# Two half quotients of a dynamic-convolution softmax, issued two places later in a hand-written schedule

## The chip, the cores and the metric

The kernel runs on one core of one Trainium2 chip. The metric is device time in microseconds (us) for one execution; lower is better. The core's engines are PE (TensorE, matmuls), DVE (VectorE), ACT (ScalarE), POOL (GpSimd) and SP (SyncE, which issues the DMAs here). Each engine works through its own list of instructions in order and waits on semaphores for the others.

## The reference

The input is x, 8 images of 256 channels by 64 x 64 pixels, fp32. Two layers follow each other, each x = x + conv(groupnorm(x)). Layer 0 is an involution: per pixel, a small network makes 9 weights for each group of 8 channels, and they weigh the pixel's 3 x 3 neighbourhood. Layer 1 adds two parts. One is attention of every pixel over its 7 x 7 neighbourhood, 4 heads, with a softmax over the 49 keys. The other is a dynamic convolution:

```python
wts = jnp.einsum('oc,bchw->bohw', Wfc, x).reshape(b, C, kc2, h, w)
wts = jax.nn.softmax(wts, axis=2)
...
out_conv = jnp.sum(oc * wts.transpose(0, 2, 1, 3, 4), axis=1)
return rate1 * out_att + rate2 * out_conv
```

All 9 branches of `oc` hold the same values, since x is broadcast over them. The weighted sum is therefore `oc` times the sum of the softmax over its 9 branches; the kernel computes that as a quotient, (the sum of 8 exponentials of differences, plus 1) times the reciprocal of the same sum.

## The kernel before, in words

**Tiling.** An image is cut into 8 bands (g counts them through all images: image b = g // 8, band i = g % 8) of 8 rows, 512 pixels. Channels lie on partitions, in two tiles of 128 (ct = 0, 1). Layer 1's work on a band is cut into 8 steps: step s has ct = s // 4 and m = s % 4. In each step the kernel

- computes attention scores of two 8 x 8 tiles of queries on PE (`scores`, L703), takes them out of PSUM with mask and maxima on DVE (L712), makes exponentials with their sums on ACT (`exponentials`, L720), inverts the sums on DVE (`probabilities`, the *small reciprocal*, L727, 128 x 2 elements) and scales the probabilities on ACT (L729);
- transposes the probabilities of the step before on PE (`transposed`, L735), copies them on ACT (L737), and multiplies those of two steps before with the values (L747); DVE adds the result to the residual (L757);
- computes two of the eight 1 x 1 convolutions for the dynamic weights on PE (`branch_weights`, L825) and their exponentials on ACT (L830); POOL sums them up (L1023);
- runs four taps of two depthwise convolutions on DVE (L782 of the first, L808 of the second; ACT starts and ends them, L773, L788, L802, L818).

Beside these, spread over the steps: the queries, keys and values of coming bands (`queries` L637, `keys` L658 with sums on DVE at L666 and L673 and a copy of old rows on POOL at L633, `values` L563, `value_tile` L607 and L609), and layer 0 some 12 bands ahead (`small_maps` L328, `value_maps` L369, `hidden_maps`, `tap_weights` with one product on DVE, L460, and one sum on POOL, L468, for each of the 9 taps).

**Order.** The order on every engine is written by hand: nothing reorders it. The main loop passes six *places* a step. `advance()` moves to the next place and runs what was put there with `after(n, f)`, n places on. In a step, the first place comes after the scores and exponentials are issued, the second after the first branch convolution and two taps, the third after the small reciprocal and the scaling, the fourth after two more taps, the fifth after the second branch convolution, the sixth after the work that is kept for the end of a step (layer 0's products are put there relative to it).

**The quotients.** When the four steps of one ct are done (at m = 3), `dynamic_sum` is put four places on, which is the second place of the next step. It adds the two halves of the exponentials' sum (L838) and 1 to it (L841) on POOL, into the tile `tot`. The quotient is made in two halves of 256 elements: DVE takes the reciprocal (`quotient`, L846) into `rec`, and one place later POOL multiplies (L847). `rec` is one buffer, which both halves use. Then `weigh` multiplies with the depthwise result and adds to the residual on POOL (L851, L852), and six places after the second ct the band is stored. For the last band's ct = 1 all of this is on DVE.

Counted in places from `dynamic_sum`, at the second place of a step with m = 0, the first half stands 7 on: the third place of the step with m = 1, just behind the small reciprocal. The second half stands 11 on: the first place of the step with m = 2. For ct = 0 these are steps 5 and 6 of the same band, for ct = 1 steps 1 and 2 of the next.

Of the kernel before, what the change touches and what calls it, by code (L numbers as in the profile page):

```python
# [86 lines left out]
def conv_layers_kernel(ctx: ExitStack, tc: tile.TileContext, ins: dict, out: bass.AP):  # L87
# [127 lines left out]
    def after(n, f):  # L215
        later.append((place[0] + n, f))
# [615 lines left out]
    def dynamic_sum(b, i, ct, ex, oc):  # L832

        tot = w1.tile([P, BAND], F32, tag="tots", name=f"tot_{b}_{i}_{ct}", bufs=1)
        xr = images[b].xr[i]

        engine = nc.vector if (b, i, ct) == (B - 1, NB - 1, NCT - 1) else nc.gpsimd
        engine.tensor_add(tot, ex[:, 1], ex[:, 0])  # L838


        engine.tensor_scalar(tot, tot, 1.0, 1.0e37, ALU.add, ALU.min)  # L841
        rec = w1.tile([P, BAND // 2], F32, tag="rec", name=f"rec_{b}_{i}_{ct}", bufs=1)

        def quotient(u):
            v = tot[:, u * BAND // 2 : (u + 1) * BAND // 2]
            nc.vector.reciprocal(rec, v)  # L846
            after(1, lambda: engine.tensor_mul(v, v, rec))  # L847

        def weigh():

            engine.tensor_mul(oc, oc, tot)  # L851
            engine.tensor_add(xr[:, ct], xr[:, ct], oc)  # L852
            if ct == NCT - 1:
                after(6, store)

        def store():
            nc.sync.dma_start(
                out=out[b].rearrange("(t p) n -> p t n", p=P)[:, :, i * BAND : (i + 1) * BAND], in_=xr
            )

        after(7, lambda: quotient(0))
        after(11, lambda: quotient(1))
        after(13, weigh)


    def beside(g, s):
# [93 lines left out]
    with tc.manual_schedule():  # L960
# [21 lines left out]
        for g in range(-AHEAD, B * NB):  # L982
            b, i = divmod(g, NB)
            for s in range(STEPS):
# [35 lines left out]
                if g >= 0:  # L1020
                    branch_weights(b, i, ct, m, 1, ex)
                    if exb is not None:
                        after(4, lambda ex=ex, exb=exb: nc.gpsimd.tensor_add(ex, ex, exb))  # L1023
                    if m == 1:
                        conv[1]()
                        conv = depthwise_middle(b, i, ct)
                    if m == NT // 2 - 1:
                        oc = depthwise_end(b, i, ct, conv[1])
                        after(4, lambda a=(b, i, ct, ex, oc): dynamic_sum(*a))
# [97 lines left out]
```

## Time and profile before

| what | value |
|---|---|
| runs shown | 4149.93 us median of 3, 4146.99 to 11589.33 |
| the profiled execution | 4146.57 us, of which the span of its instructions 4144.8 us |
| busy share of PE, DVE, ACT, POOL | 97%, 82%, 75%, 76% |
| the half quotients L846 | 256 of 1742 ns, DVE idle 123.7 us ahead of them |
| the small reciprocals L727 | 512, median 159 ns |
| POOL's multiplies L847 | 254 of 730 ns, POOL idle 326.6 us ahead of them |
| granted clock of PE, mean | 0.990 |

A group's row of the page reads: line, engine, operation, what it writes and reads, how many | busy us, mean ns of one | idle time of its engine just before, and what ended most of it. A row of the waits reads: who waited, for whom, total us, times, longest us. A row of the order of time reads: start in us from the span's start, duration, engine, line, and in brackets the engine's idle time before it. A row of the windows reads: stretch, its length, then busy us and instructions of PE, PE's weight loads, DVE, ACT and POOL, then PE's granted clock, the DMAs' share and GB/s. PE's starts are measured and its ends are modelled, so its gaps are best read from start to start.

### The profile page before, as it was taken

Reading aid. Unit: us, or ns where it says so; the run is one execution under the profiler, and the core shown is the slowest. Engines: PE = TensorE matmul, PEld = TensorE weight load, DVE = VectorE, ACT = ScalarE, POOL = GpSimd, SP = SyncE. Lnnn points to the kernel's source line nnn. Section 1 sums busy time; section 2 is a strip of 40 time slices with the busy share of each in tenths; the row PEclk is TensorE's granted clock in tenths of the full one; section 3 lists DMA queues with packets and bytes.
Section 4 is the critical chain, followed back from the end, with each engine's and each line's share of the span. In section 5 each row is a group of like instructions: output and inputs, shape, how many; then the busy total and the mean of one; then the engine's idle time right before and its main releaser. Section 6 shows DMA issues by size and latency. Waiting matters only on the chain.

```text
span 4144.8 us, 72568 instructions
## 1 busy us (share of the span) xinstructions
PE 4025.7 (97%) x25292; PEld 2134.1 (51%) x25292; DVE 3414.6 (82%) x7090; ACT 3092.9 (75%) x7758; POOL 3170.8 (76%) x2156
## 2 busy tenths in 40 slices
PE   6889999999999999999999999999999999999998
PEld 2345555555555555555555555555555555555554
DVE  5778888788888888888888888888888788877777
ACT  3467778778777777877778777777778777687776
POOL 4768888788887888878887878878888788855555
PEclk9999999999999999999999999999999999999999
DMA  8853333333343433433433433342433332111100
GB/s 225 193 138 89 95 91 96 83 97 88 84 100 81 103 94 78 100 96 82 98 85 83 105 97 81 89 103 77 99 84 81 79 90 73 41 46 39 39 28 21
DMA packets 381262, 367.87 MB, mean 89 GB/s; under 512 B 55648, under 2 KB 282720, under 8 KB 380640
## 3 DMA queue, kind: packets, MB, share of 16 engines
q1 hardware_dynamic: 377568, 358.68, 34.6%
q8 instruction: 200, 3.28, 0.3%
q10 hardware_dynamic: 3328, 4.55, 0.3%
q14 instruction: 166, 1.36, 0.1%
HBM read 261.42 MB, written 101.71 MB: 88 GB/s over the span
## 4 chain that ended last, share of the span: by engine, by line
PE 44%; POOL 21%; DVE 19%; ACT 7%; issue 5%; DMA 2%; SPq 2%; POOLq 0%; DVEq 0%; ACTq 0%
PE pf L825 20%; POOL xg L468 9%; DVE rec L846 6%; POOL ex L1023 5%; DVE prod L460 5%; PE sco L747 3%; PE pk L658 3%; PE ptp L735 3%; PE sco L703 3%; PE p L369 2%; PE pq L637 2%; DVE acc L782 2%; DVE acc L808 2%; POOL tot L841 2%; PE pvt L607 2%
## 5 line engine op out<-in xcount | busy, mean ns | idle before, releaser
L825 PE MATMUL pf<-yp,c_wfc 128*128 128x512 f32 x4096 | 1935.2, 596 | 11.0 <-ACT vc L581 5.3
L468 POOL TENSOR_TENSOR xg<-xg,prod 128x1024 f32<-128x1024 f32 x549 | 1200.8, 2187 | 377.6 <-DVE prod L460 357.6
L825 PEld LDWEIGHTS pf<-yp,c_wfc 128*128 128x128 f32 x4096 | 733.2, 191 | 693.4 <-issue 596.8
L1023 POOL TENSOR_TENSOR ex<-ex,ex 128x1024 f32<-128x1024 f32 x384 | 908.0, 2365 | 110.0 <-ACT ex L830 105.8
L782 DVE SCALAR_TENSOR_TENSOR acc<-yp,c_chan,acc 128x504 f32<-128x504 f32 (+3 forms) x1104 | 765.2, 693 | 48.7 <-ACT acc L773 28.2
L460 DVE SCALAR_TENSOR_TENSOR prod<-pw,c_par,x3q 128x1040 f32<-128x1040 f32 x576 | 733.0, 1279 | 69.4 <-PE pw L447 24.6
L808 DVE SCALAR_TENSOR_TENSOR acc<-hid,c_chan,acc 128x504 f32<-128x504 f32 (+3 forms) x1024 | 756.7, 739 | 18.1
L830 ACT ACTIVATE ex<-pf 128x512 f32<-128x512 f32 x1024 | 604.1, 590 | 207.3 <-PE pf L825 192.4
L729 ACT ACTIVATE prob<-prob,tot 128x196 f32<-128x196 f32 x1024 | 411.9, 452 | 356.1 <-DVE tot L727 356.0
L712 DVE CUSTOM_DVE_ANT_0 prob<-sco,c_mask 128x196 f32<-128x196 f32 x1024 | 326.3, 356 | 272.4 <-PE sco L703 271.4
L846 DVE RECIPROCAL rec<-tot 128x256 f32<-128x256 f32 x256 | 446.1, 1742 | 123.7 <-POOL tot L841 123.7
L720 ACT ACTIVATE prob<-prob,nmax 128x196 f32<-128x196 f32 x1024 | 461.1, 454 | 16.4 <-DVE nmax L712 14.9
L847 POOL TENSOR_TENSOR tot<-tot,rec 128x256 f32<-128x256 f32 x254 | 185.5, 730 | 326.6 <-DVE rec L846 326.6
L747 PEld LDWEIGHTS sco<-pt,vt 112*64 112x64 f32 x8160 | 283.9, 137 | 182.1 <-issue 62.8
L737 ACT COPY pt<-ptp 112x512 f32<-112x512 f32 x511 | 296.2, 580 | 105.3 <-PE ptp L735 102.1
L747 PE MATMUL sco<-pt,vt 112*64 112x64 f32 x8160 | 347.4, 227 | 0.0
L735 PE MATMUL ptp<-ident,prob 128*112 128x128 f32 x2044 | 339.8, 288 | 6.7 <-ACT prob L729 5.8
L703 PE MATMUL sco<-kb,qb 64*64 64x196 f32 x4096 | 296.7, 359 | 0.0
L735 PEld LDWEIGHTS ptp<-ident,prob 128*112 128x112 f32 x2044 | 206.6, 134 | 169.4 <-issue 94.9
L841 POOL TENSOR_SCALAR tot<-tot 128x512 f32<-128x512 f32 x127 | 243.6, 1918 | 11.1
L563 PE MATMUL pv<-yp,c_wv 128*128 128x512 f32 (+2 forms) x576 | 246.8, 553 | 0.0
L369 PE MATMUL p<-xc,w3s 128*128 128x512 f32 x512 | 244.8, 602 | 0.0
(140 smaller groups left out, 5165.1 us busy)
## 6 DMA issues: line engine op xcount, KB each, us to landing
x<-x3n SPq DMA_DIRECT2D x128, 264.0 KB, 2.1
x3q<-x SPq DMA_DIRECT2D x128, 264.0 KB, 7.4
xc<-in_x SPq DMA_DIRECT2D x64, 512.0 KB, 5.2
xg<-in_x SPq DMA_DIRECT2D x256, 128.0 KB, 5.1
x<-xg SPq DMA_DIRECT2D x256, 128.0 KB, 2.4
yp<-x SPq DMA_DIRECT2D x128, 256.0 KB, 3.3
xr<-x SPq DMA_DIRECT2D x64, 512.0 KB, 6.1
out_x<-xr SPq DMA_DIRECT2D x64, 512.0 KB, 3.1
```

Of the source, the lines that this page charges most:

```text
L460: nc.vector.scalar_tensor_tensor(prod[:, :, :RUN], pw[:, j, :RUN].unsqueeze(1).to_broadcast([P, SHARE, RUN]), par[:, PCB2 + k : PCB2 + k + 1],
L468: nc.gpsimd.tensor_add(im.xg[i], im.xg[i], rows(prod))
L703: nc.tensor.matmul(sco[half[t], h, :NKEY], qb[half[h], 2 * m + t].rearrange("p r c -> p (r c)"), kb[half[h], :, c0 : c0 + KW], start=True, ...
L720: nc.scalar.activation(prob[:, h, :NKEY], prob[:, h, :NKEY], AF.Exp, bias=nmax[:, h : h + 1], scale=-1.0, accum_out=tot[:, h : h + 1],)
L735: nc.tensor.transpose(ptp[:, h, ch], prob[:, h, ch * CHUNK : (ch + 1) * CHUNK], ident)
L747: nc.tensor.matmul(po[half[h], :, t * TQ : (t + 1) * TQ], im.vt[i + ch, m][:n, t, (2 * ct + h) * HD : (2 * ct + h + 1) * HD], pt[:n, h, ch ...
L782: nc.vector.scalar_tensor_tensor(o, yp[:, ct, ra + dr : rb + dr, ca + dc : cb + dc], chan[:, ct, CW1 + k : CW1 + k + 1], o, ALU.mult, ALU.add,
L808: nc.vector.scalar_tensor_tensor(o, hid[:, ra + dr : rb + dr, ca + dc : cb + dc], chan[:, ct, CW2 + k : CW2 + k + 1], o, ALU.mult, ALU.add,)
L825: nc.tensor.matmul(pf, wfc[:, kt, 2 * m + j, ct * P : (ct + 1) * P], images[b].yp[i][:, kt, PAD : PAD + R], start=(kt == 0), stop=(kt == N ...
L830: nc.scalar.activation(ex[:, j].rearrange("p (r c) -> p r c", r=R), pf, AF.Exp)
L846: nc.vector.reciprocal(rec, v)
L1023: after(4, lambda ex=ex, exb=exb: nc.gpsimd.tensor_add(ex, ex, exb))
```

## The change

The first half goes from 7 to 9 places, the second from 11 to 13, and `weigh` from 13 to 15. The first half is then issued after the last two taps of the step with m = 1, the second after the small reciprocal of the step with m = 2.

```diff
-        after(7, lambda: quotient(0))
-        after(11, lambda: quotient(1))
-        after(13, weigh)
+        after(9, lambda: quotient(0))
+        after(13, lambda: quotient(1))
+        after(15, weigh)
```

On DVE, in a step with m = 1 and the one with m = 2 behind it:

```
before                                    after
L727 small reciprocal (m = 1)             L727 small reciprocal (m = 1)
L846 half quotient 0                      L782 taps, 2
L782 taps, 2                              L846 half quotient 0
L460 product (where one stands)           L460 product (where one stands)
L712 mask and maxima, L757 (m = 2)        L712 mask and maxima, L757 (m = 2)
L846 half quotient 1                      L460 product (where one stands)
L460 product (where one stands)           L808 taps, 2
L808 taps, 2                              L727 small reciprocal (m = 2)
L727 small reciprocal (m = 2)             L846 half quotient 1
L808 taps, 2                              L808 taps, 2
```

## The prediction

> **What bounds the kernel now.** I read the page first (busy shares, costliest groups), then who waited for whom, then PE's order of time in single steps, last DVE's and ACT's order of time ahead of PE's gaps. In the names below image b and band i count from 0, and a band has steps 0 to 7 (step s is ct = s // 4, m = s % 4).
>
> ```profile
> PE 4025.7 (97%) x25292; PEld 2134.1 (51%) x25292; DVE 3414.6 (82%) x7090; ACT 3092.9 (75%) x7758; POOL 3170.8 (76%) x2156
> L846 DVE RECIPROCAL rec<-tot 128x256 f32<-128x256 f32 x256 | 446.1, 1742 | 123.7 <-POOL tot L841 123.7
> ACT prob L729 <- DVE tot L727: 356.0, 267, 3.2
> PE pvt L607 <- ACT ex L830: 14.6, 6, 2.4
> ```
>
> PE is the bound: 97% busy, and DVE, ACT and POOL have 18 to 25% to spare. So an edit on DVE is worth only what it takes out of PE's few gaps. The second line says that DVE stood still 123.7 us ahead of the half quotients, waiting for POOL's sum; the third that ACT's scaling of the probabilities waited 356 us for the small reciprocal (L727); the fourth that PE waited six times, 2.4 us each, for an exponential of ACT.
>
> The same step (step 7, one of band 4, one of band 3 of image 3) with and without a gap, PE's order of time, start and duration:
>
> ```profile
> 2051.07 0.58 PE L703 MATMUL sco<-kb,qb 64*64 64x196 f32 x8
> 2051.78 0.78 PE L735 MATMUL ptp<-ident,prob 128*112 128x128 f32 x4
> 2052.70 1.98 PE L825 MATMUL pf<-yp,c_wfc 128*128 128x512 f32 x4
> 2054.52 1.88 PE L658 MATMUL pk<-yp,c_wk 128*128 128x512 f32 x4
> 2059.97 0.57 PE L703 MATMUL sco<-kb,qb 64*64 64x196 f32 x8
> ...
> 1990.68 0.58 PE L703 MATMUL sco<-kb,qb 64*64 64x196 f32 x8
> 1991.18 0.65 PE L735 MATMUL ptp<-ident,prob 128*112 128x128 f32 x4
> 1991.67 1.88 PE L825 MATMUL pf<-yp,c_wfc 128*128 128x512 f32 x4
> 1998.83 0.57 PE L703 MATMUL sco<-kb,qb 64*64 64x196 f32 x8
> ```
>
> From score to score the first takes 8.90 us, the second 8.15 us, with the same instructions. The 0.75 us lie around the transposes L735, which need the probabilities of step 6: 0.21 us ahead of them, 0.43 us between their halves, 0.10 us after. What DVE and ACT did just before the slow one:
>
> ```profile
> 2039.16 0.16 DVE L727 RECIPROCAL tot<-tot 128x2 f32<-128x2 f32 x1
> 2041.79 1.75 DVE L846 RECIPROCAL rec<-tot 128x256 f32<-128x256 f32 x1 [2.48 <-POOL tot L841]
> 2043.46 1.46 DVE L782 SCALAR_TENSOR_TENSOR acc<-yp,c_chan,acc 128x512 f32<-128x512 f32 x2
> 2044.83 1.29 DVE L460 SCALAR_TENSOR_TENSOR prod<-pw,c_par,x3q 128x1040 f32<-128x1040 f32 x1
> 2046.86 1.74 DVE L846 RECIPROCAL rec<-tot 128x256 f32<-128x256 f32 x1
> 2048.52 1.20 DVE L460 SCALAR_TENSOR_TENSOR prod<-pw,c_par,x3q 128x1040 f32<-128x1040 f32 x1
> 2051.08 0.16 DVE L727 RECIPROCAL tot<-tot 128x2 f32<-128x2 f32 x1
> ...
> 2051.27 0.81 ACT L729 ACTIVATE prob<-prob,tot 128x196 f32<-128x196 f32 x2 [3.12 <-DVE tot L727]
> ```
>
> The first half quotient holds DVE for 2.48 us with two ready taps behind it; the second stands ahead of the small reciprocal; ACT waits 3.12 us for that one, and PE's transposes wait for ACT. The chain that ended last has these same pieces (rec L846 is 6% of it).
>
> [...] the taps at 2043.46 needed nothing and stood behind the waiting reciprocal. [...]
>
> ```profile
> 2235.26 0.65 PE L607 MATMUL pvt<-ident,vc 128*112 128x128 f32 x4 [2.42 <-ACT ex L830]
> 2230.50:2235.20 4.70, 2.34 (x10) 1.08 (x8) 4.66 (x10) 1.53 (x5) 3.28 (x3) 1.00 0.00 0
> 2237.20:2241.20 4.00, 4.00 (x13) 2.15 (x10) 3.96 (x10) 1.63 (x6) 3.84 (x4) 0.66 0.00 0
> ```
>
> The column after the five engines is the granted clock: 0.66 just after the gap. [...] The moved reciprocal reads one, and POOL's L468 takes 2.17 to 2.19 us beside it and away from it; I cost contention at nothing.
>
> **The change part by part.** The built order shows that PE, ACT and SP keep their instructions in the same order (so every DMA issue too). On DVE only the 256 half quotients move; on POOL the second multiply (L847) goes behind the copy of keys L633 where one stands there. Nothing is added or removed.
>
> *First half.* It goes from ahead of two taps to behind them, still ahead of the product L460. In steps 5 the taps (1.46 us) run in what was a wait: 2.48 - 1.46 leaves a wait of 1.0 us, and everything behind (product, mask, scores' maxima of step 6) comes up to 1.46 us earlier. In steps 1 DVE did not wait for POOL, the sum is the same, and nothing behind moves. POOL's first multiply then ends later by 1.46 us in steps 1, but the next thing in POOL's queue, the sum L468, waits for the product, which takes 1.29 us against the multiply's 0.73: nothing.
>
> *Second half.* It goes behind the product, two taps and the small reciprocal: 1.74 us less ahead of L727. L727 cannot run before ACT's exponentials end. They ended 3.5 us before it in steps 6, 1.8 us in steps 2 (from the order of time), so the whole 1.74 us comes in steps 6, about 1.65 in steps 2. Together L727 of step 6 comes about 3.2 us earlier, where PE needs 0.75. What is behind it now (two taps, key sums L666) has the same work ahead of it as before. The quotient itself ends about 2.9 us later, less in steps 6; POOL's second multiply used to start 5.7 us after it, since POOL was busy with L468 and L1023, and even after their advance by at most 1.7 us some 1 us is left.
>
> *Sum on PE.* (a) Step 7, bands 1, 2, 4, 5 of images 0 to 5: 24 x 0.75 = 18.0 us. (b) Step 7 of band 0, images 0 to 6, read off in the same way: 7 x 0.55 = 3.9. (c) Image 6, step 7 of bands 1 to 3: 3 x 0.77 = 2.3; bands 4 and 5 show 1.5 and 2.4, of which I take 3. (d) Step 3 (behind the quotient in step 2) of bands 3 and 6: 13 x 0.37 = 4.8 of excess, part of it not at the transposes; between 0 and 4.8 I take 3. (e) Band 7, step 6, six images: L727 was at 2233.72; without 1.74 and the taps' 1.19 (two of 384) it is at about 2230.8, ACT's exponential behind it at about 2232.3 instead of 2234.63, limited then by PE's own matmul; the gap of 2.42 shrinks to some 0.2. The half clock after it goes too: (1 - 0.66) x 4.0 = 1.36 and 0.17 x 2.0 = 0.34 in the two us ahead (clock 0.83), 1.7; I take 1.6. 6 x (2.2 + 1.6) = 22.8. Together 18.0 + 3.9 + 2.3 + 3 + 3 + 22.8 = 53 us. Not touched: step 5 of band 0 (1.3 us an image), where DVE is behind by plain work. Tail: the last group divides in the old order; the group before it finishes on POOL 1.3 us later, beside 1.5 us of idle POOL time ahead of the last L1023: 0.
>
> The profiled execution took 4146.57 us (span 4144.8 and 1.8 around it): 4146.6 - 53 = 4094. The median of the runs shown, 4149.93, is 3.4 above it: 4097.
>
> **Rivals.** *Given back in part*: the transposes come free, but PE, ahead by 0.75 us a band, meets the next wait (POOL's sum still holds DVE 1.0 us in steps 5, ACT's 192 us of waiting for PE shows how tight PE and ACT run), and band 7 keeps its clock dip. Half of (a) to (d), none of (e) but a little: about 25 us, 4125. Against it: the other steps' probabilities come 1.5 us or more ahead of the transposes after the change.
> *Nothing*: the late probabilities come from something else, for instance the copy of pt, and the moved wait is hidden: 4148. Against it: band 3, whose step 5 waits for POOL 0.45 us instead of 2.5, has no gap.
> *Slower*: the second quotient used to fill DVE's time while ACT made the exponentials. Behind L727 it no longer does, and taps and key sums come late. It decides in steps 2 and 6 from the point where the exponentials end over 1.74 us later against DVE than now (the margins are 1.8 and 3.5). Price: up to 1.74 us in each of two steps; bands with idle DVE time (step 0 alone has 1.5 us) absorb it, bands 0, 3, 6, 7 (32) would pay about 1 us and the gains fall away: 4150 + 32 = 4182.
>
> **How the numbers follow.** Forecast 0.70 (its own range 4084 to 4110), given back in part 0.16, nothing 0.08, slower 0.06. Beyond all of it, PE's other excess is small: removing every gap that I found would give some 70 us, 4080, which is the low end. The high end, 4135, takes in the second case. 2% is 83 us, about what a measurement of this kernel can tell from no change; no case reaches that except by surprise, so faster 0.03, same 0.95, slower 0.02.
>
> **What would show it.** Right: L846's wait for POOL about halved (123.7 to some 60), ACT's wait for L727 down from 356 by 200 or more, steps 7 of bands 1, 2, 4, 5 at 8.15 us, no 2.4 us wait of L607 and no clock dip in band 7. Wrong: steps 7 still at 8.9, L727 waiting for ACT far longer than 117.5 us, or POOL's L847 waiting more in its second half.

## The result and the profile after

The changed kernel takes 4091.20 us (median of 4 runs, 4090.07 to 4094.71), the kernel before 4149.97. The ratio is 0.9862, with a 95% interval of 0.9843 to 0.9882: 1.4% faster, inside the 2% on either side of no change in which the prediction put it. The forecast was 4097. (Among the runs of before one of 11589 us stands apart; the ratio leaves it out.) The profiled execution went from 4146.57 to 4094.71 us, 51.9 less, where the prediction's sum was 53. A later group of runs on another chip gave 53.0 us between the medians, so the 58.8 us here hold some scatter.

From the page of the changed kernel and its waits (who waited, for whom, total us, times, longest):

```profile
PE 3995.2 (98%) x25292; PEld 2128.2 (52%) x25292; DVE 3413.2 (83%) x7090; ACT 3115.3 (76%) x7758; POOL 3174.3 (78%) x2156
L846 DVE RECIPROCAL rec<-tot 128x256 f32<-128x256 f32 x256 | 445.4, 1740 | 14.0 <-POOL tot L841 13.9
ACT prob L729 <- DVE tot L727: 164.1, 256, 1.6
DVE tot L727 <- ACT prob L720: 117.6, 82, 2.1
POOL tot L847 <- DVE rec L846: 456.3, 98, 11.3
```

DVE has the same work (445 us of half quotients), but its wait ahead of them fell from 123.7 to 14.0 us and ACT's wait for the small reciprocal from 356 to 164. (The instructions of all engines are the same in number. ACT's busy time is higher than before because its records overlap less: added up one by one they take 3641.5 us, before 3639.6. PE's is lower, since its modelled ends take in some waiting: the transposes L735 read 0.78 us in the slow step above and 0.65 below.) The small reciprocal itself waits no longer for ACT than before (117.5 then). POOL's multiply waits longer than before (326.6 then); no loss of PE shows for it. PE's wait for ACT's exponential ahead of L607, 14.6 us before, is 1.5 us, 0.3 at most.

PE's order of time in the same step 7 of band 4, image 3, and around the former gap in band 7:

```profile
2026.85 0.58 PE L703 MATMUL sco<-kb,qb 64*64 64x196 f32 x8
2027.35 0.65 PE L735 MATMUL ptp<-ident,prob 128*112 128x128 f32 x4
2035.00 0.57 PE L703 MATMUL sco<-kb,qb 64*64 64x196 f32 x8
...
2207.10 0.65 PE L607 MATMUL pvt<-ident,vc 128*112 128x128 f32 x4 [0.25 <-ACT ex L830]
2208.30:2215.20 6.90, 6.90 (x59) 4.10 (x56) 5.65 (x15) 4.69 (x12) 6.74 (x6) 1.00 0.02 5
```

The step is 8.15 us long instead of 8.90, with the transposes right behind the scores. In band 7, 0.25 us is left of the 2.42 us gap, and the granted clock in the step behind it (last line, a stretch of the windows view) is 1.00.

What DVE did in steps 5 and 6 of band 4:

```profile
2015.06 1.54 DVE L782 SCALAR_TENSOR_TENSOR acc<-yp,c_chan,acc 128x512 f32<-128x512 f32 x2
2016.51 1.75 DVE L846 RECIPROCAL rec<-tot 128x256 f32<-128x256 f32 x1
...
2023.73 0.16 DVE L727 RECIPROCAL tot<-tot 128x2 f32<-128x2 f32 x1
2023.81 1.73 DVE L846 RECIPROCAL rec<-tot 128x256 f32<-128x256 f32 x1
```

The first half follows the taps with no wait at all, and the small reciprocal of step 6 starts 3.1 us ahead of the scores of step 7 (2026.85); before, it started at 2051.08, with them (2051.07).

Read in this way from the first score of the main loop to that of its last step, the loop takes 3822.7 us instead of 3876.2, 53.5 less; the stretch ahead of it was 1.5 longer in this execution. (Over all the traces of this case that stretch, which no version changes, takes between 245.1 and 253.2 us.)

### The profile page after: what moved, and what is told of

It is laid out like the page before. It is cut to its first block, busy times and chain, and to the rows that moved or that the text cites. A ratio compares the mean times of both kernels' runs of the same rounds, so it can differ in the third digit from the quotient of the medians.

```text
span 4092.9 us, 72555 instructions
## 1 busy us (share of the span) xinstructions
PE 3995.2 (98%) x25292; PEld 2128.2 (52%) x25292; DVE 3413.2 (83%) x7090; ACT 3115.3 (76%) x7758; POOL 3174.3 (78%) x2156
## 4 chain that ended last, share of the span: by engine, by line
PE 81%; DVE 7%; POOL 5%; ACT 3%; issue 2%; DMA 2%; SPq 1%; POOLq 0%; ACTq 0%; DVEq 0%
PE pf L825 37%; PE sco L747 6%; PE ptp L735 6%; PE sco L703 5%; PE pq L637 5%; PE p L369 5%; PE pk L658 4%; PE pv L563 4%; PE pvt L607 3%; PE pw L447 2%; POOL xg L468 2%; DVE prod L460 2%; DVE acc L808 1%; PE p L328 1%; POOL ex L1023 1%
## 5 line engine op out<-in xcount | busy, mean ns | idle before, releaser
L468 POOL TENSOR_TENSOR xg<-xg,prod 128x1024 f32<-128x1024 f32 x549 | 1200.0, 2186 | 164.4 <-DVE prod L460 135.6
L782 DVE SCALAR_TENSOR_TENSOR acc<-yp,c_chan,acc 128x504 f32<-128x504 f32 (+3 forms) x1104 | 774.0, 701 | 41.7 <-ACT acc L773 21.2
L847 POOL TENSOR_TENSOR tot<-tot,rec 128x256 f32<-128x256 f32 x254 | 185.6, 731 | 463.6 <-DVE rec L846 456.3
L846 DVE RECIPROCAL rec<-tot 128x256 f32<-128x256 f32 x256 | 445.4, 1740 | 14.0 <-POOL tot L841 13.9
L735 PE MATMUL ptp<-ident,prob 128*112 128x128 f32 x2044 | 332.0, 285 | 0.0
L735 PEld LDWEIGHTS ptp<-ident,prob 128*112 128x112 f32 x2044 | 206.4, 133 | 152.7 <-issue 109.6
L841 POOL TENSOR_SCALAR tot<-tot 128x512 f32<-128x512 f32 x127 | 243.6, 1918 | 11.1
L563 PE MATMUL pv<-yp,c_wv 128*128 128x512 f32 (+2 forms) x576 | 245.7, 551 | 1.0 <-DVE prod L460 1.0
```

The costliest lines, as they stand in the source:

```text
L468: nc.gpsimd.tensor_add(im.xg[i], im.xg[i], rows(prod))
L735: nc.tensor.transpose(ptp[:, h, ch], prob[:, h, ch * CHUNK : (ch + 1) * CHUNK], ident)
L782: nc.vector.scalar_tensor_tensor(o, yp[:, ct, ra + dr : rb + dr, ca + dc : cb + dc], chan[:, ct, CW1 + k : CW1 + k + 1], o, ALU.mult, ALU.add,
```

## The experiments

Theory: PE's gaps were set by DVE's time (work and waits) in front of the small reciprocal of steps 6 and 2. Rivals: only the second half's place counts; or only the wait for POOL; or the clock dips for a reason of its own. All ratios are to the kernel before, in runs on the same chip; its medians there were 4146.5 us (beside the first half alone, the second half alone, band 7 alone and all but band 7), 4147.1 (beside the two buffers and the three kernels with more time) and 4146.4 (beside the last four).

**The first half alone.**

```diff
-        after(7, lambda: quotient(0))
+        after(9, lambda: quotient(0))
```

> Only the first half is moved (9, 11, weigh 13). Queue-time theory: what counts is DVE time ahead of the small reciprocal in steps 6; PE lacks some 0.3 us at its transposes there, the first half alone gives about 1.46 us, so steps 7 of bands 1, 2, 4, 5 fall to 8.15 us as with both; steps 3 of bands 3 and 6 keep their excess; in band 7 the gap of 2.42 us shrinks by the taps' 1.19 to about 1.2, with or without the clock dip behind it: 34 to 44 us off, 4106 to 4116. Rival, second half alone does it: a wait for POOL is only put elsewhere, 4140 to 4150.

4118.24 us, ratio 0.9934 (0.9919 to 0.9948): 28 us off, less than expected. Steps 7 of bands 1 and 2 did fall to 8.16 us, so the first half alone frees the transposes there. But bands 4 and 5 came down only to 60.77 and 60.52 us (from 61.16, against 60.40 with both halves moved), band 7 to 63.7 in most images, and the clock still dipped (to 0.5 for 3.41 us) in five of six images. The waits name a new one:

```profile
DVE rec L846 <- POOL tot L841: 50.5, 42, 3.2
DVE rec L846 <- POOL tot L847: 20.6, 42, 1.0
```

The first row is mostly the expected 1.0 us that is left of each 2.5 us wait; in band 7 it is 3.2 of 4.4. The second is one that the change as a whole doesn't have: the halves are now two places apart instead of four, they share one buffer, and the second must wait until POOL has multiplied with the first.

**The first half alone, with two buffers.**

```diff
-        rec = w1.tile([P, BAND // 2], F32, tag="rec", ..., bufs=1)
+        recs = [w1.tile([P, BAND // 2], F32, tag=f"rec{u}", ..., bufs=1) for u in range(2)]
```

The first half stands 9 places on, as in the run above.

> The first half alone moved, but the two halves use two buffers for their reciprocals. In the run with one buffer the second half waited 20.6 us for POOL's first multiply to read it. If that wait is what the first half alone lost in bands 4, 5 and 7: it vanishes, bands 4 and 5 come down from 60.77 and 60.52 to 60.4 us, band 7's gap shrinks by about 0.6 us: 4104 to 4112. If POOL's sum is what holds it: no change, 4118.

4102.08 us, 0.9896 (0.9881 to 0.9910). The wait on L847 is gone, bands 4 and 5 take 60.40 us, band 7 61.45, and no clock dip is left in the main loop: the shared buffer had cost the first half 16 us, over a third of the 45 that it can bring. This also came out 2 us better than the expectation's best. POOL's sum still held DVE 50.7 us here, so this gain does not come from an earlier sum. (In the kernel before no half waits for L847, so that a second buffer alone has no wait to remove there; it was not run.)

**The second half alone.**

```diff
-        after(11, lambda: quotient(1))
-        after(13, weigh)
+        after(13, lambda: quotient(1))
+        after(15, weigh)
```

> Only the second half is moved (7, 13, weigh 15). Queue-time theory: 1.74 us less ahead of the small reciprocal clears steps 7 and 3 alone; band 7's gap shrinks from 2.42 to about 0.7 and its clock dip goes: about 50 us off, 4100. The gains of the two halves alone then add up to far more than that of both (59 us). Rival, the wait for POOL at the first half is what matters: under 20 us off, 4130 or more.

4099.04 us, 0.9887 (0.9873 to 0.9902), as the theory had it. All bands but band 0 take what they take with both halves moved (60.40, 60.45 in band 7); band 0 is 68.0 us instead of 66.8, longer even than the 67.3 of the kernel before. So each half frees PE nearly alone: 45 us (with two buffers) and 47 us against 53 to 59 for both. The gains don't add up, because in most bands PE needs only 0.75 us and either half gives more.

**Band 7 alone, and all but band 7.**

```diff
+        on = 2 if (i, ct) == (NB - 1, 0) else 0
+        after(7 + on, lambda: quotient(0))
+        after(11 + on, lambda: quotient(1))
+        after(13 + on, weigh)
```

The second kernel has 0 and 2 the other way round.

> Both halves are moved for band 7, ct = 0 alone (its steps 5 and 6). Theory: six gaps of 2.4 us and six clock dips of 1.6 us go, 6 x 3.8 = 23 us off, 4127, and no half-rate stretch of the clock in the main loop. Rival, the clock dips once an image for another reason: only the gaps go, 13 us off, 4137, and the dips stay.

> Both halves are moved everywhere but for band 7, ct = 0. If the parts add up: 59 - 23 = 36 us off, 4114, with the clock dip once an image still there. If band 7's gap came from work pushed on by the bands ahead of it, it shrinks too and the time is 4100 or less.

Band 7 alone: 4130.34 us, 0.9961 (0.9947 to 0.9975), 16 us off. Band 7 falls from 64.3 to 60.5 us in six images, 3.8 each as expected, and the six half-rate stretches of the clock (granted 0.50 for 3.41 us each in the kernel before) are gone from the main loop: they followed the gap. But band 0 behind it grew from 67.3 to 68.7 us, and this line of PE's order of time shows where:

```profile
2237.36 3.70 PE L563 MATMUL pv<-yp,c_wv 128*128 128x512 f32 x8 [1.00 <-ACT vt L609]
```

PE came to the next image's first step earlier than ACT, and some 1.4 us an image were given back. All but band 7: 4099.47 us, 0.9889 (0.9875 to 0.9904), 47 us off, where 36 had been expected if the parts add up. Its band 7 takes 61.25 us without being touched:

```profile
2212.83 0.65 PE L607 MATMUL pvt<-ident,vc 128*112 128x128 f32 x4 [1.07 <-ACT ex L830]
```

The gap is 1.07 instead of 2.42 us, and the clock does not dip.

Why it shrank shows in POOL's order of time ahead of the sum, in band 4 of image 3, first before, then after the change:

```profile
2018.98 2.18 POOL L468 TENSOR_TENSOR xg<-xg,prod 128x1024 f32<-128x1024 f32 x1 [1.47 <-DVE prod L460]
2039.84 1.92 POOL L841 TENSOR_SCALAR tot<-tot 128x512 f32<-128x512 f32 x1
...
1991.08 4.45 POOL L468 TENSOR_TENSOR xg<-xg,prod 128x1024 f32<-128x1024 f32 x2 [0.39 <-DVE prod L460]
2014.36 1.92 POOL L841 TENSOR_SCALAR tot<-tot 128x512 f32<-128x512 f32 x1
```

In step 2 POOL waited 1.47 us for a product that stood on DVE behind the second half of ct = 1. From there to the sum L841 it has no gap, in either kernel. Without the second half in step 2 the two sums run back to back, and L841 ends 1.29 us earlier in its step (4.24 us behind the first score of step 5 instead of 5.53, read in image 3's band 2). That is what the first half of ct = 0 waits for, three steps later. The other kernels bear it out: in the same band L841 ends 4.26 us behind that score with the second half alone moved, 5.55 and 5.52 with the first half alone (one buffer and two). In band 7 it ends 6.48 us behind instead of 7.83, in the all-but-band-7 kernel as in the changed one.

**More time in front of the small reciprocal.** The changed kernel with one or two reciprocals of 256 elements added for ct = 0 (their results are not used): in one kernel ahead of the product, as below; in the others behind the taps (place 12), once or twice.

```diff
+        if ct == 0:
+            more = w1.tile([P, BAND // 2], F32, tag="more", ..., bufs=1)
+            after(11, lambda: nc.vector.reciprocal(more, w3[:, 0, :]))
```

> The changed kernel, with one more reciprocal of 256 elements on DVE (of a weight tile; its result is not used) in each band's step 6, at the place that the second half left: ahead of the product. Queue-time theory: the small reciprocal of steps 6 is late by 1.74 us again, of 2.6 us to spare; POOL gets its product late, and the wait of the first half for POOL comes back (some 1 us in steps 5). No gap in steps 7 of bands 1 to 6; band 7 loses up to 12 us: 4095 to 4105. Theory that only the second half's own place counts (its dependence on POOL): 4091.

> The same with the added reciprocal behind the product and two taps, just ahead of the small reciprocal. The small reciprocal is late by the same 1.74 us, but POOL's product is not: the wait for POOL stays near the 14 us of the changed kernel. If what is left in band 7 is due to the small reciprocal alone, the time is that of the run before this; if POOL's earlier product carries part of the gain, it is faster than that one: 4092 to 4102.

> Two such reciprocals there (3.5 us). They exceed the 2.6 us to spare by 0.9: PE's transposes of steps 7 wait again, by about 0.9 us and 0.45 around them, in some 35 steps, and band 7 gets its gap of 2.4 us or more and its clock dip back: 45 + 30 us on top of 4091, 4150 to 4170. If DVE's order does not set PE's gaps: 4091 to 4105.

One, ahead of the product: 4105.73 us, 0.9904 (0.9888 to 0.9921). One, behind product and taps: 4106.23, 0.9906 (0.9891 to 0.9920). Steps 7 stay at 8.15 us in both, as expected with 2.6 us to spare (in the changed kernel ACT's scaling ends at 2024.74, the transposes begin at 2027.35). But the two agree, and the wait of the first half for POOL is 13.8 us in both, so the expectation that it would come back with a late product in step 6 was wrong: it is the product of step 2 that counts, and nothing was added there. What the two lose is band 0 (68.4 us instead of 66.8 from its first scores), which neither expectation had in it, and 0.7 us in band 7.

Two behind the taps: 4180.13 us, 1.0083 (1.0068 to 1.0098), slower than before and more than expected. PE's gap is back, from 2061.53 to 2070.70 us, 9.17 us for step 7 of band 4:

```profile
2062.52 0.78 PE L735 MATMUL ptp<-ident,prob 128*112 128x128 f32 x4 [0.42 <-ACT prob L729]
```

So 1.7 us fit in front of the small reciprocal, and 3.5 do not. POOL's sum is as early here as in the changed kernel (DVE waits 13.8 us for it), so it is DVE's time in front of the small reciprocal that brings PE's gap back, and not the wait for POOL. Step 7 lost 1.0 us where 1.35 was expected; what was underrated is that it met nearly every band (61.4 us instead of 60.4), not 35 steps, and that band 0 lost 2.8 us an image. Band 7 lost less than expected: its gap came back at 1.72 us, not 2.4, and the clock dipped in one image of six.

**A further version.** For ct = 1, DVE waits 1.7 us for ACT in step 1, and POOL 5.8 us for the first half: room for both halves, one step earlier than the second now stands.

```diff
+        q0, q1, w = (6, 9, 12) if ct else (9, 13, 15)
```

The other two runs put the halves of band 7, ct = 0 later still, `(11, 15, 17)`, alone and together with this; the fourth is the changed kernel once more.

> The changed kernel once more, to compare the next three with on one chip: 4091.

> The changed kernel, but for ct = 1 the halves stand earlier: 6 and 9 places on, weigh 12 (all in the next band's step 1), where DVE waits 1.7 us for ACT's exponentials and POOL 5.8 us for the first half. ct = 0 as changed. Queue-time theory: band 0 is short of DVE time from step 2 on (its transposes of step 5 wait 1.1 us); with the second half out of step 2 and the first in idle time, about 1.0 us of the 1.2 us around step 5 goes in six images, and POOL's sum for ct = 0 comes earlier too, which helps band 7: 4078 to 4086. If band 0's gap is not DVE's backlog: 4091.

> The changed kernel, but for band 7, ct = 0 the halves stand later still (11, 15, weigh 17), so that DVE does not wait the last 1.9 us for POOL's sum in step 5. Theory: the 0.5 us that are left of the gap in step 6 and part of the 0.3 us in band 0's step 0 go: 3 to 5 us, 4086 to 4088. If the first half in front of the small reciprocal of step 6 costs what it did: 4095 or more.

> Both of these together. If the two gaps are separate the gains add up: 4076 to 4083. If the earlier POOL sum has taken the wait in band 7 already, it is as fast as with ct = 1 early alone.

The changed kernel gave 4093.37 us here (0.9869, 0.9853 to 0.9884; runs 4088.28 to 4096.14). ct = 1 early: 4086.57 us (0.9855, 0.9842 to 0.9869; runs 4084.23 to 4087.70). That is 6.8 us less, just short of what was expected (4086 at most). The intervals of the ratios overlap, the runs don't, and the traces differ where they should, PE in step 5 of band 0, first the changed kernel, then this one:

```profile
2259.66 0.70 PE L735 MATMUL ptp<-ident,prob 128*112 128x128 f32 x4
2261.26 1.98 PE L825 MATMUL pf<-yp,c_wfc 128*128 128x512 f32 x4 [0.89 <-ACT vc L581]
...
2254.20 0.65 PE L735 MATMUL ptp<-ident,prob 128*112 128x128 f32 x4
2254.83 1.98 PE L825 MATMUL pf<-yp,c_wfc 128*128 128x512 f32 x4
```

From the transposes to the next matmul it is 0.63 instead of 1.60 us; six images have it, 5.8 of the 6.8 us. DVE's wait for ACT ahead of the small reciprocal fell with it, from 119.8 to 33.0 us: it is filled now. POOL's sum for ct = 0 did come earlier, by 0.8 us in band 7, but band 7 stayed at 60.45 us: that part of the expectation failed. It is the fastest of the versions.

Band 7 late was a loss: 4113.77 us, 0.9925 (0.9912 to 0.9937), and 4107.55 us, 0.9907 (0.9893 to 0.9920), together with the early ct = 1; neither of the expected gains came. The wait for POOL in step 5 did go, and band 7 stayed at 60.45 us; but 15 places on, the second half stands in front of the mask of step 7, and what hangs on that mask had nothing to spare:

```profile
2215.60 1.75 DVE L846 RECIPROCAL rec<-tot 128x256 f32<-128x256 f32 x1 [0.61 <-POOL tot L847]
2218.39 0.35 DVE L712 CUSTOM_DVE_ANT_0 prob<-sco,c_mask 128x196 f32<-128x196 f32 x1
2226.34 5.40 PE L563 MATMUL pv<-yp,c_wv 128*128 128x512 f32 x8 [1.98 <-ACT vt L609]
```

The scores of step 7 had started at 2214.61, the mask follows 3.8 us later (1.4 in the changed kernel), and with it the last taps of the image, ACT's work behind them (L818 at 2222.14, L773 at 2222.86, L788 at 2224.83, L609 at 2225.71), and at last PE, 1.98 us late in band 0. Band 0 is longer by 2.3 us in two images and by 3.7 in four. In the four the clock dipped behind this gap, as in the line of L563 above, where eight matmuls take 5.40 us (3.70 in the kernel with band 7 alone); in the trace of the two together, with the same gaps, it dipped in none. That is the same place where the band-7-only kernel gave time back.

## Why the prediction was right, point by point

- *What bounds the kernel*: right. PE's late starts, and the half clock behind one of them (0.50 for 3.41 us an image, in six), were the whole of it; the loop lost 53.5 us with every engine's instructions unchanged.
- *(a)*, 24 steps 7: 18.0 predicted; bands 1, 2, 4, 5 went from 61.16 to 60.40 us, 24 x 0.76 = 18.3.
- *(b)*, band 0: 3.9 predicted, about 3.4 measured (67.28 to 66.84 in most images).
- *(c)*, image 6: 2.3 + 3 predicted; 2.3 for bands 1 to 3, and 1.45 and 2.40 in bands 4 and 5, so all of those two and not a part.
- *(d)*, steps 3: 3 predicted out of 4.8; band 3 went from 62.48 to 62.27 us and band 6 from 59.53 to 59.31, in six images each, together 2.7. Image 6, the thirteenth of the count, gained nothing there.
- *(e)*, band 7: 22.8 predicted; 64.3 to 60.45 us, six times 3.8 = 22.9, of which 2.2 in step 6 and 1.6 in step 7, as predicted. The clock dip went with the gap, and the band-7-only kernel shows that it followed it.
- *The wait for POOL*: wrong in size. "In steps 5 the taps run in what was a wait: ... leaves a wait of 1.0 us" held for the first half alone (50.5 us in all). With the second half moved too, 14.0 us were left, not some 60: the second half of ct = 1 also frees POOL's products in step 2, and POOL's sum comes 1.3 us earlier. The prediction left the time of that sum as it was; it let POOL's work come earlier only where it asked whether the second multiply would wait. In most bands PE had no use for this last microsecond, so the error left the sum right, which is luck; only band 7 shows it (61.25 instead of 64.3 us in the all-but-band-7 kernel).
- *That the parts add up within the sum*: the sum was right for both halves together (53.5 us measured in the loop, against 53), with small errors of either sign in (b), (c) and (d), where the sizes were in part picked between limits. The text says that 3.2 us come where PE needs 0.75, but not what follows from it: that either half is nearly enough.
- *The signs named*: the steps 7 and band 7 came as named. ACT's wait for L727 fell by 192 us, a little short of "200 or more". One sign of being wrong did appear: POOL's multiply of the second half waited more, 35.2 us in all instead of 15.2. Nothing of PE's time went with it. The second multiply of most bands still starts about 2 us after its reciprocal has ended (5.7 before; 1 was predicted).
- *Rivals*: "given back in part" is not what the change did, but it is what band 7 alone did, in band 0. "Slower" (DVE idle behind an uncovered wait) didn't happen: L727's wait for ACT is 117.6 against 117.5 us. *Nothing* is excluded: the steps 7 came down when the probabilities came earlier, and rose again when DVE was given more in front of the small reciprocal.
- *The tail and contention*: right. From the last step's first score to the end of the span it is 18.83 us instead of 18.71. POOL's L468 takes 2186 ns in the mean (2187 before) and the half quotient 1740 (1742), so these means show no contention.

## What to carry to other kernels

Where one engine is 97% busy, look for the few steps that take longer than the same step elsewhere, and follow that one wait back through the queues: here that of DVE, where two ready taps stood behind a half quotient that waited 2.48 us, and the small, urgent reciprocal (0.16 us) behind a long one (1.74 us) that nobody waited for. Put the long, unurgent instruction behind the urgent one and in front of as little as possible; then check what it holds up two and three steps later, on other engines too (products, buffers, the first work of the next image). Before moving a second piece, measure each alone: gains that clear the same slack do not add up, and two instructions that share one buffer need their distance kept.

## What the runs showed of the hardware that was not expected

In these traces the granted clock of PE fell to 0.5 behind some pauses of PE of 1.72 to 2.44 us, and their length alone does not decide it. Counted in band 7 and the band 0 behind it, where each dip lasted 3.41 us:

| pause of PE, us | where | images with a dip |
|---|---|---|
| 2.4 | band 7, kernel before | 6 of 6 |
| 1.98 | band 0, band 7 late | 4 of 6 |
| 1.98 | band 0, early and late | 0 of 6 |
| 1.9 | band 7, first half alone | 5 of 6 |
| 1.72 | band 7, two behind the taps | 1 of 6 |
| 1.6 and less | band 0, two behind the taps, and the other traces | none |

In the trace of the kernel before, the six dips begin 1.1 to 1.5 us after the pauses end. They follow each other at 498.35 us, which is 146 times 3.413 us. In this trace and in that of the changed kernel the starts of all stretches at half clock, those ahead of the main loop too, lie whole multiples of 3.413 us apart, to within 0.03 us. What made the difference between the pauses of 1.98 us with a dip and those without was not shown. Nor was it shown how many dips another execution would have: each kernel with such pauses has one trace here.
